# Order and engines of the first image's blocks in a convolution by codebooks: means before shuffles, a patch set before later loads, one pair of numerators on VectorE, one map half through GpSimd's queue

## The chip, the cores and the metric

One core of a Trainium2 chip. The metric is the device time of one execution in microseconds, as the median of several runs. TensorE (PE in the profile), VectorE (DVE), ScalarE (ACT) and GpSimd (POOL) compute; SyncE (SP) only issues transfers. Each engine works through its own instructions in the order in which the program lists them.

## The reference

`x` is 16 images of 256 channels, 28 x 28, in fp32. Cut to what matters:

```python
def amm_conv3x3(x, centroids, w_sub):          # per channel: 16 centroids of 9 values
    p = ...                                    # 3x3 patches: image, position, channel, 9
    d = |p|^2 - 2 p.centroids + |centroids|^2  # distance to 16 centroids of this channel
    attn = softmax(-d)                         # over the 16
    lut = einsum('cks,cso->cko', centroids, w_sub)
    return einsum('bnck,cko->bno', attn, lut)

h = _gn(x)                                     # group norm, 32 groups
out = relu(bn1(amm_conv3x3(h, centroids1, w_sub1)))
out = bn2(amm_conv3x3(out, centroids2, w_sub2))
out = se_layer(out)                            # gate per channel
return x + relu(out + h)
```

## The kernel before, in words

The softmax and the table are taken apart: for each channel the exponentials of the logits are summed against the 9 centroid values (numerators) and against one (denominators), each numerator is multiplied by the reciprocal of its denominator, and the result, 9 values for each channel, goes through an ordinary product with `w_sub`. An image of a layer is four **blocks**: two halves of the channels times two halves of the rows (`BLOCKS`, L46). Two layers of 16 images give 128 blocks, numbered `j` in order; block 0 to 3 are the first image's first layer.

For a block:

- `patches` (L388) loads the shifted rows from a padded map in DRAM, `home1` in the first layer. A block has two patch sets, `p` = 0 and 1, each of six transfers. Sets are counted over all blocks, so the tenth is block 4's second. Two buffers hold them (`pts`; block 1 uses the space of weight slabs, seen as `wall<-home`).
- `logits` (`lg`, L409) and `exps` (`e`, L420): four groups `mm` of a block, TensorE and ScalarE.
- `num_b` (`nb`, L474): the denominators and the ninth numerator. `split_r`, `join_r` (L484, L488), `recip_dve` (L502) make the reciprocal `r`; `split_q`, `join_q` (L494, L499) the ninth numerator.
- `spread` (L513, L517) shuffles `r` to the numerators' rows on VectorE: two shuffles for a group, one for the ninth.
- `num_a` (`na`, L460): the other numerators, one PSUM pair a group. `scale_a` (L536) multiplies them by the spread reciprocals on VectorE, straight from PSUM. Groups in `kept` instead go by `copy_a` (L530, ScalarE) and `scale_q` (L525, GpSimd).
- `product` (L544) multiplies slices `k` of the result by a weight slab, 392 columns at a time. A fp32 matmul is two passes in the profile. The four products of an image's blocks are combined as a seven-multiplication scheme, with `mix` (L551, L553) on GpSimd for its sums and `combine` (L226) for its weights.

Four PSUM pairs of banks are handed on by written rotation (`ROLES`) and, for the first three blocks, by a written table (`EARLY`). A matmul that writes a bank waits for the engine that read it before.

The image's own path: `load_x` reads it into `xt`, one buffer; `gn_stats` (L339, L340) takes the statistics on VectorE; `gn_mean` and `gn_var` each need one small matmul (`gnp`, L345 and L362) and a few VectorE steps (L349 to L353, L364); GpSimd finishes with `rsqrt` (L276, L277) and two steps (L367, L368); `gn_apply` (L374) normalises on ScalarE into `xpads[k]`, where `k` is the half of the channels; `to_home1` (L386) writes it to `home1`, two copies shifted by one. Half 1 of a map is first read by the third block of that image.

The order is written out by hand. `at(cl, sub, f, ...)` files a step under a key, and all steps are issued in the order of the keys; every engine takes its own instructions from that one list. Steps with negative keys are the start. A block's work takes two numbers of `cl`; block 4 begins at 8. Keys that the change touches, before:

- image 1: `load_x` (0, 1.65), `gn_stats` (3, 1.3), block 1's shuffles for groups 1, 2, 3 (3, 1.40 to 1.43), block 0's product in three pieces of 4, 2 and 3 slices (4, 0.80), (4, 0.82), (4, 0.84), with `gn_mean` (4, 0.81) and `gn_var` (4, 0.83) between them;
- block 1's scalings (4, 1.04 on), its kept group 0 copied at (4, 1.05) and scaled on GpSimd at (5, 0.08);
- image 1's `to_home1`: half 0 at (4, 1.6), half 1 at (6, 1.6);
- image 2: `load_x` (6, 2.6), `gn_stats` (8, 0.3); block 3's `join_r` stands at (8, 1.2), its scalings at (9, 1.04);
- block 4's patch sets at (6, 1.5) and (7, 1.5).

Of the kernel before, what the change touches and what calls it, by code (L numbers as in the profile page):

```python
# [17 lines left out]
P = 128  # L18
# [21 lines left out]
SLOT_MM = (1, 0, 2, 3)  # L40
# [43 lines left out]
def kernel(  # L84
# [20 lines left out]
    nc = tc.nc  # L105
# [39 lines left out]
    home1 = [dram.tile([C, 2, HROW], F32, name=f"home1_{b}") for b in range(B)]  # L145
# [116 lines left out]
    xpads = [io.tile([P, NPAD], F32, tag="pc", name="xpad", bufs=4) for _ in range(NB)]  # L262
# [116 lines left out]
    def twice(t):  # L379
        return view(t, 0, [t.ap[0], [1, 2], [1, HROW]])  # L380

    def to_home1(b, k, half=None):
        if k == NB - 1:
            xs.pop(b)
        p0, p1 = (0, P) if half is None else (64 * half, 64 * half + 64)
        nc.sync.dma_start(home1[b][k * P + p0 : k * P + p1], twice(xpads[k][p0:p1]))  # L386

    def patches(u, p):  # L388
        hm = (home1 if u["l"] == 0 else home2)[u["b"]]
# [532 lines left out]
    def at(cl, sub, f, *a, **kw):  # L922
        jobs.setdefault((cl, sub), []).append((f, a, kw))

    def wide_next(j):
        return j + 1 < len(blocks) and blocks[j + 1]["l"] == 1 and blocks[j + 1]["hh"] == 0
# [7 lines left out]
    for j, u in enumerate(blocks):  # L934
        gi, g = 8 * (j // 4), 2 * j
# [12 lines left out]
    for j, u in enumerate(blocks):  # L948
        g = 2 * j
        u["w"] = j  # L950
        wide = u["l"] == 1 and u["hh"] == 0
        for p in range(2):
            u["pt", p] = alts[p] if j == 1 else pts[p]
            if j == 1:
                at(-0.4 if p else -0.9, 0.0, patches, u, p)
            else:
                at(g + p - (2 * NPT if j == 2 else NPT), 1.5, patches, u, p)
            for q in range(2):
                mm = 2 * p + q
                cl, sub = TURN.get((j, mm), (g + p, 0.1 + (0.2 * q if j < 3 else q)))  # L960
                at(cl, sub, logits, u, mm)
                if wide and mm == 0:
                    at(g, 0.12, wide_copy, u, mm)
                    at(g, 0.9, wide_turn, u, mm)
                    at(g, 1.38, wide_max, u, mm)
                    at(g, 1.39, wide_sub, u, mm)
                    at(g + 1, 1.22, wide_back, u, mm)
                    at(g + 1, 1.89, wide_exp, u, mm)
                else:
                    at(cl, 1.06 if (cl, sub) == (4, 1.035) else sub + 0.01, exps, u, mm)  # L970
        kept = SLOT_MM[1 : 4 if wide_next(j) or j == 0 else 2 : 2]
        g = 2 * j + 1 + (j > 2)
        at(g, 1.0, num_b, u)
        at(g, 1.05, split_r, u)
        at(g, 1.2, join_r, u)
        at(g, 1.25, recip_dve, u)
        at(g, 1.3 if j > 1 else 1.06, split_q, u)
        at(g, 1.35 if j > 1 else 1.21, join_q, u)
        g = 2 * j + 2 + (j > 1)
        for i, mm in enumerate(SLOT_MM):  # L980
            at(g, 1.0 + 0.01 * i, num_a, u, mm)
            if mm in kept:
                at(g, 1.05, copy_a, u, mm)
            else:
                at(g - 1, 2.05 if i == 4 - len(kept) and j > 1 else 1.4 + 0.01 * i, spread, u, mm)
                at(g, 1.04 + 0.001 * i, scale_a, u, mm)
        for mm in (4, *kept):
            at(g, 1.2, spread, u, mm)
            at(*((g, 1.3) if j != 1 else (5, 0.06 if mm == 4 else 0.08)), scale_q, u, mm)

    for l in range(2):
        for b in range(B):
            n = l * B + b
            g = 8 * n
            us = blocks[4 * n : 4 * n + 4]
            for c, w, r, ks in PRODUCTS:
                if g + c == 5:
                    for sub, k0, k1 in ((0.8, 0, 4), (0.82, 4, 6), (0.84, 6, 9)):
                        at(4, sub, product, (n, c), us[r], w, ks[k0:k1], k0 == 0, k1 == 9, step=4)
                else:  # L1000
                    at(g + c, 2.0, product, (n, c), us[r], w, ks, step=g + c)
            for mm in (1, 2, 3, 4, 0):
                at(g + 5, 2.5 if n else {4: 0.07, 0: 0.09}.get(mm, 0.05), mix, us[0], mm, us[1], us[0])
                at(g + 7, 1.35 if mm in (4, 0) else 1.25, mix, us[1], mm, us[2], us[1])
                at(g + 8, 1.37 if mm == 1 else 1.4, mix, us[0], mm, us[2], us[0])
                at(g + 10, 1.4, mix, us[0], mm, us[0], us[3])
            c11, c12, c21, c22 = (0, 0), (0, 1), (1, 0), (1, 1)
            at(*((g + 6, 0.0) if n else (4, 0.85)), acc_copy, l, b, c11, (n, 5))
            at(g + 6, 2.02, acc_copy, l, b, None, (n, 6))
            at(g + 8, 0.0, acc_add, l, b, None, (n, 7))  # L1010
            at(g + 8, 2.02, acc_add, l, b, c21, (n, 8), c11)
            at(g + 10, 0.0, acc_add, l, b, c22, (n, 9), c11, pop=False)
            at(g + 10, 0.01, acc_add, l, b, c21, (n, 9))
            at(g + 10, 0.05, reg_add, l, b, c12, c22, None)
            at(g + 10, 0.06, reg_add, l, b, c22, c21, None)
            at(g + 10, 2.02, acc_add, l, b, c12, (n, 10))
            at(g + 12, 0.0, acc_add, l, b, c11, (n, 11))
            at(g + 12, 2.02, acc_add, l, b, c21, (n, 12), op=ALU.subtract)
            if l == 0 or b == B - 1:
                at(g + 11, 1.9, norm_out, l, b, *c12)  # L1020
                at(g + 11, 1.91, norm_out, l, b, *c22)
                at(g + 12, 1.9 if l else 0.05, norm_out, l, b, *c11)
                at(g + 13, 1.06, norm_out, l, b, *c21)
            else:
                for o in range(NB):
                    at(g + 12 + o, 1.9, norm_both, b, o)
            if l == 0:
                for o in range(2):
                    if b == 0:
                        at(g + 13, 1.9, rank_score, o)  # L1030
                        at(g + 13, 1.91, rank_keep, o)
                        at(g + 12 + 2 * o, 0.65 if o else 1.93, h0_keep, o)
                    else:
                        for r in range(2):
                            at(g + 12 + o + (o and r), (0.06, 1.97)[r] if o == 0 else (1.805, 2.9)[r], to_home2, b, o, r)
                if b + 1 < B:
                    at(*((g - 2, 2.6) if b else (0, 1.65)), load_x, b + 1)
                    for q in range(NB):
                        at(*((g, 0.3) if b else (3, 1.3)), gn_stats, b + 1, q)
                    at(*((g + 1, 2.1) if b else (4, 0.81)), gn_mean, b + 1, step=g + 1 if b else 4)  # L1040
                    at(*((g + 3, 2.1) if b else (4, 0.83)), gn_var, b + 1, step=g + 3 if b else 4)
                    for q in range(NB):
                        at(*((g + 4, 1.9) if b else (4, (0.95, 1.055)[q])), gn_apply, b + 1, q)
                        at(*((g + 4, 1.92) if b else (4 + 2 * q, 1.6)), to_home1, b + 1, q)
            else:
                last = b == B - 1
                at(*((g + 11, 0.6) if last else (g + 13, 2.6)), load_x, b, last)
                at(g + 14 - last, 2.1, se_hidden, b, g + 14 - last)
                at(*((g + 14, 1.05, se_gate, b, g + 14) if last else (g + 17, 2.1, se_gate, b, g + 17)))
                at(*((g + 14, 1.05) if last else (g + 18, 0.3)), se_recip, b)  # L1050
                for q in range(NB):
                    at(*((g + 12, 0.4) if last else (g + 19, 1.9)), finish_norm, b, q)
                    if not last:
                        at(g + 18, 1.9, finish_gate, b, q)
                        at(g + 20, 0.05, finish_sum, b, q)
                        at(g + 20, 1.9, finish_relu, b, q)
                        at(g + 20, 2.2, finish_add, b, q)
                        at(g + 20, 2.25, store, b, q)
                    else:
                        at(g + 14, 1.92, finish_fast, b, q)  # L1060
                        at(g + 14, 1.92, store, b, q)
                if b == B - 1:
                    at(g + 11, 1.9, flags)
                    at(g + 12, 2.9, flag_sum)
# [49 lines left out]
    g = 8 * B  # L1114
# [23 lines left out]
    for i in range(2):  # L1138
        to_home1(0, 0, i)
# [18 lines left out]
    with tc.If(rv > 0):  # L1158
        with tc.For_i(0, B, 1) as it:
# [14 lines left out]
            for l in range(2):  # L1174
# [6 lines left out]
                for t2 in range(2):  # L1181
                    us = []
                    for hh in range(2):
                        u = {"l": l, "b": B, "t": t2, "hh": hh, "w": 0, "step": None}
# [127 lines left out]
```

## Time and profile before

| | |
|---|---|
| median of 3 runs | 2630.71 us (2627.92 to 2631.47) |
| profiled execution | 2632.19 us |
| its span, first to last instruction | 2630.7 us |
| TensorE matmul busy | 2587.2 us, 98% |
| VectorE, ScalarE, GpSimd busy | 67%, 52%, 72% |
| mean granted TensorE clock | 0.997 |

A row of a timeline gives start, duration, engine, source line, operation, output<-inputs, shape, count; the bracket at the end is the idle time of the engine before it and what ended it. `gn_st` are the statistics, `gnp` the group matmuls, `qp` and `qo` the numerators (pairs and the ninth), `rb` the spread reciprocals, `xt` the image, `home<-xpad` the map's write, `pt<-home` and `wall<-home` the patches. SPq is SyncE's queue. Neighbouring instructions of one form are merged, with their count.

### The profile page before, as it was taken

What the parts mean: (1) busy time and instruction counts of PE and PEld (TensorE: products, weight loads), DVE (VectorE), ACT (ScalarE), POOL (GpSimd) and SP (SyncE); (2) the same over time, 40 slices, a digit from 0 to 9 for tenths busy, and PEclk for the clock granted to TensorE, in tenths of its full rate; (3) what the DMA queues carried; (4) which work ended last, traced back from release to release, by engine and by line L of the source; (5) the groups of instructions that cost most, each with busy time, mean ns of one, the idle gap of its engine ahead of it and who ended that gap; (6) DMA issues with size and microseconds to landing.
All of it is one profiled execution on the core that took longest, in us unless ns stands there. A gap on an engine that the chain in (4) does not pass through costs nothing.

```text
span 2630.7 us, 85667 instructions
## 1 busy us (share of the span) xinstructions
PE 2587.2 (98%) x36984; PEld 1267.9 (48%) x36984; DVE 1766.0 (67%) x3759; ACT 1360.6 (52%) x1876; POOL 1902.8 (72%) x1320
## 2 busy tenths in 40 slices
PE   6999999999999999999999999999999999999997
PEld 2444454444544445444444444444444444444444
DVE  5776566666567665666666776767776667767665
ACT  4444444445444444444454555555555655555653
POOL 3876667766667766677667777778878787777786
PEclk9999999999999999999999999999999999999999
DMA  8656655665455566655664444444444444444441
GB/s 209 163 154 180 186 162 162 189 182 165 140 147 146 175 184 173 173 151 154 169 168 107 111 116 117 127 115 117 106 126 128 118 118 110 117 119 125 114 121 47
DMA packets 217831, 374.37 MB, mean 142 GB/s; under 512 B 29752, under 2 KB 188008, under 8 KB 217448
## 3 DMA queue, kind: packets, MB, share of 16 engines
q1 hardware_dynamic: 211272, 336.16, 47.8%
q0 software_dynamic: 6176, 32.66, 3.4%
q8 instruction: 295, 4.83, 0.8%
q14 instruction: 88, 0.72, 0.1%
HBM read 288.93 MB, written 79.80 MB: 140 GB/s over the span
## 4 chain that ended last, share of the span: by engine, by line
PE 96%; DMA 2%; DVE 1%; POOL 0%; ACT 0%; SPq 0%; issue 0%; DVEq 0%; POOLq 0%; ACTq 0%
PE acc L544 52%; PE lg L409 17%; PE na L460 14%; PE nb L474 13%; DMA xt<-in_x 1%; DMA wall<-home 1%; DMA pt<-home 0%; PE sep L846 0%; DVE gn_st L339 0%; DVE rb L517 0%; SPq L395 0%; DMA home<-xpad 0%; POOL qp L553 0%; PE sep L835 0%; PE gnp L362 0%
## 5 line engine op out<-in xcount | busy, mean ns | idle before, releaser
L544 PE MATMUL acc<-qp,wall 128*128 128x392 f32 x3072 | 1096.8, 500 | 1.7 <-POOL qp L553 0.9
L420 ACT ACTIVATE e<-lg 128x784 f32<-128x784 f32 x960 | 738.0, 821 | 638.2 <-PE lg L409 635.1
L553 POOL TENSOR_TENSOR qp<-qp,qp 128x784 f32<-128x784 f32 x512 | 944.9, 1869 | 158.6 <-DVE qp L536 158.1
L544 PEld LDWEIGHTS acc<-qp,wall 128*128 128x128 f32 x3072 | 565.2, 190 | 509.1 <-issue 55.3
L517 DVE STREAM_SHUFFLE rb<-r 128x392 f32<-128x392 f32 x1024 | 551.0, 605 | 0.0
L409 PE MATMUL lg<-pt,wd 32*32 32x392 f32 x16256 | 483.4, 502 | 7.3 <-DMA pt<-home 2.7
L488 DVE SCALAR_TENSOR_TENSOR r<-nb,kst,r 128x392 f32<-128x392 f32 x128 | 80.0, 625 | 452.6 <-ACT r L484 438.8
L536 DVE TENSOR_TENSOR qp<-na,rb 128x784 f32<-128x784 f32 x351 | 333.0, 972 | 64.7 <-PE na L460 53.7
L460 PE MATMUL na<-e,cwa 64*32 64x392 f32 x8192 | 374.8, 492 | 0.7 <-DVE hpad L581 0.7
L474 PE MATMUL nb<-e,cwb 64*32 64x392 f32 x8192 | 374.8, 493 | 0.1
L525 POOL TENSOR_TENSOR qo<-qo,rb 128x392 f32<-128x392 f32 x128 | 131.3, 1026 | 314.1 <-DVE rb L513 313.6
L502 DVE RECIPROCAL r<-r 128x392 f32<-128x392 f32 x128 | 333.2, 2603 | 4.4
L525 POOL TENSOR_TENSOR qp<-qp,rb 128x784 f32<-128x784 f32 x161 | 297.9, 1860 | 2.9
L474 PEld LDWEIGHTS nb<-e,cwb 64*32 64x32 f32 x8192 | 192.4, 107 | 174.3 <-issue 19.5
L460 PEld LDWEIGHTS na<-e,cwa 64*32 64x32 f32 x8192 | 182.9, 106 | 183.5 <-issue 76.2
L409 PEld LDWEIGHTS lg<-pt,wd 32*32 32x32 f32 x16256 | 121.2, 103 | 283.1 <-issue 252.1
L544 PE MATMUL acc<-qp,w_A 128*128 128x392 f32 x512 | 183.9, 502 | 0.0
L484 ACT ACTIVATE r<-nb,kst 128x392 f32<-128x392 f32 x128 | 86.7, 677 | 164.0 <-PE nb L474 164.0
L444 POOL TENSOR_TENSOR z<-z,mx 128x1568 f32<-128x1568 f32 x32 | 91.8, 2869 | 94.7 <-DVE mx L438 94.7
L544 PE MATMUL acc<-qo,wall 128*128 128x392 f32 x384 | 157.7, 492 | 0.0
L530 ACT COPY qp<-na 128x784 f32<-128x784 f32 x161 | 130.8, 812 | 27.0 <-PE na L460 25.2
L544 PEld LDWEIGHTS acc<-qp,w_A 128*128 128x128 f32 x512 | 95.0, 191 | 83.0 <-DVE qp L536 19.8
(154 smaller groups left out, 1646.8 us busy)
## 6 DMA issues: line engine op xcount, KB each, us to landing
pt<-home SPq DMA_DIRECT2D x762, 209.0 KB
pt<-home SPq DMA_DIRECT2D x762, 104.5 KB
home<-xpad SPq DMA_DIRECT2D x31, 899.0 KB
xt<-in_x SPq DMA_DIRECT2D x30, 784.0 KB
out_dram<-y SPq DMA_DIRECT2D x32, 392.0 KB
d_wS<-st SPq DMA_DIRECT2D x12, 192.0 KB
wall<-d_wS SPq DMA_DIRECT2D x4, 576.0 KB
wall<-in_ws SPq DMA_DIRECT2D x3, 576.0 KB
```

The costliest lines, as they stand in the source:

```text
L409: nc.tensor.matmul(bk[32 * c : 32 * c + 32, :N].rearrange("p (r w) -> p r w", w=W), lhsT=wts["wd", u["hh"]][32 * i : 32 * i + 32, mm, c, : ...
L420: nc.scalar.activation(eg[:, 2 * i : 2 * i + 2, :], bk[:, :, :N], AF.Exp, scale=2.0)
L444: nc.gpsimd.tensor_tensor(zk, zk, mx.unsqueeze(2).to_broadcast([P, N // 4, K]), ALU.subtract)
L460: nc.tensor.matmul(bs[32 * i : 32 * i + 32, r, :N], lhsT=wts["cwa", u["hh"]][64 * r : 64 * r + 64, mm, i, :], rhs=es[64 * r : 64 * r + 64, ...
L474: nc.tensor.matmul(bs[32 * i : 32 * i + 32, r, :N], lhsT=wts["cwb", u["hh"]][64 * r : 64 * r + 64, mm, i, :], rhs=es[64 * r : 64 * r + 64, ...
L502: nc.vector.reciprocal(u["r"], u["r"])
L517: nc.vector.stream_shuffle(rb[:, r, :], u["r"], mask_of(2 * mm + r))
L525: nc.gpsimd.tensor_tensor(q, q, u.pop(("rb", mm)), ALU.mult)
L530: nc.scalar.copy(pair(u, mm), u.pop(("na", mm))[:, :, :N])
L536: nc.vector.tensor_mul(pair(u, mm), u.pop(("na", mm))[:, :, :N], rb)
L544: nc.tensor.matmul(accs[key][:, :N], lhsT=wl[w][:, k, :], rhs=us["q", k], start=first and n == 0, stop=last and n == len(ks) - 1,)
L553: nc.gpsimd.tensor_tensor(pair(out_u, mm), pair(in0, mm), pair(in1, mm), ALU.subtract)
```

## The change

- `to_home1(0, 1)`, the first image's half 1, is issued by GpSimd instead of SyncE. Its place in the list, before block 1's patches, is unchanged.
- Block 1 keeps no group: group 0 is scaled by VectorE from PSUM like the other three, and its copy on ScalarE and its scaling on GpSimd go. Its two shuffles, which stood after the scalings, join the others.
- Block 1's shuffles move behind the second image's `gn_mean` (group 1's) and behind `gn_var` (the others).
- Block 0's product is cut into 5, 2 and 2 slices.
- The third image's `load_x` moves behind the tenth patch set, and its `gn_stats` from before block 3's `join_r` to just before block 3's scalings.
- Half 1 of the second map is written behind that load.

```diff
@@ to_home1
-        nc.sync.dma_start(home1[b][k * P + p0 : k * P + p1], twice(xpads[k][p0:p1]))
+        eng = nc.gpsimd if (b, k) == (0, 1) else nc.sync
+        eng.dma_start(home1[b][k * P + p0 : k * P + p1], twice(xpads[k][p0:p1]))
@@ blocks
-        kept = SLOT_MM[1 : 4 if wide_next(j) or j == 0 else 2 : 2]
+        kept = () if j == 1 else SLOT_MM[1 : 4 if wide_next(j) or j == 0 else 2 : 2]
...
-                at(g - 1, 2.05 if i == 4 - len(kept) and j > 1 else 1.4 + 0.01 * i, spread, u, mm)
+                if j == 1:
+                    at(4, 0.835 if i else 0.815, spread, u, mm)
+                else:
+                    at(g - 1, 2.05 if i == 4 - len(kept) and j > 1 else 1.4 + 0.01 * i, spread, u, mm)
...
-            at(*((g, 1.3) if j != 1 else (5, 0.06 if mm == 4 else 0.08)), scale_q, u, mm)
+            at(*((g, 1.3) if j != 1 else (5, 0.06)), scale_q, u, mm)
@@ products
-                    for sub, k0, k1 in ((0.8, 0, 4), (0.82, 4, 6), (0.84, 6, 9)):
+                    for sub, k0, k1 in ((0.8, 0, 5), (0.82, 5, 7), (0.84, 7, 9)):
@@ images
-                    at(*((g - 2, 2.6) if b else (0, 1.65)), load_x, b + 1)
+                    at(*((g - 2 + (b == 1), 2.6 - (b == 1)) if b else (0, 1.65)), load_x, b + 1)
                     for q in range(NB):
-                        at(*((g, 0.3) if b else (3, 1.3)), gn_stats, b + 1, q)
+                        at(*((g + (b == 1), 0.3) if b else (3, 1.3)), gn_stats, b + 1, q)
...
-                        at(*((g + 4, 1.92) if b else (4 + 2 * q, 1.6)), to_home1, b + 1, q)
+                        at(*((g + 4, 1.92) if b else (4 + 3 * q, 1.6 + 0.05 * q)), to_home1, b + 1, q)
```

## Prediction

> **What bounds the kernel now.** I read the busy times by stretch first, then the chain that ended last, then each engine's timeline where these two pointed.
>
> ```profile
> 24.00:50.00 26.00, 20.80 (x481) 7.39 (x450) 12.15 (x33) 16.17 (x22) 5.17 (x4) 0.93 0.89 210
> 50.00:80.00 30.00, 26.84 (x369) 11.93 (x347) 21.99 (x53) 13.83 (x20) 14.30 (x12) 0.94 0.79 200
> 80.00:110.00 30.00, 26.64 (x413) 12.21 (x398) 19.79 (x43) 12.10 (x16) 28.95 (x17) 1.00 0.73 198
> 110.00:2580.00 2470.00, 2468.21 (x35528) 1212.40 (x35534) 1675.64 (x3556) 1294.88 (x1787) 1803.28 (x1235) 1.00 0.52 142
> ```
>
> In a row by stretch the second number is TensorE's busy time, the last three are granted clock, DMA share and GB/s. From 110 to 2580 us TensorE stands still for 1.79 us of 2470: nothing can be gained there, and what TensorE gains before 110 us it keeps to the end, since the engines behind it follow it. Before 110 us it stands still for 5.20, 3.16 and 3.36 us, and the diff touches only work between 20 and 110 us. The first two of these rows also show a granted clock below 1.0. So the whole question is which of some 12 us of holes close. The chain names what they hang on.
>
> ```profile
> 10.37 4.15 DMA home<-xpad
> ...
> 42.94 11.03 DMA xt<-in_x
> ...
> 56.36 3.05 DVE rb L517 x6
> ...
> 80.36 12.99 DMA xt<-in_x
> ```
>
> Twice it is an image being loaded, and once six shuffles that stand on VectorE between that image's statistics and its group means.
>
> **Part 1: means ahead of the shuffles, and a longer first piece of the product.** TensorE around 52 to 69 us, in order:
>
> ```profile
> 52.31 2.90 PE L544 MATMUL acc<-qp,w_A 128*128 128x392 f32 x8
> 56.47 0.39 PE L345 MATMUL gnp<-gn_mv,gmat 128*128 128x4 f32 x2 [1.26 <-DVE gn_mv L340]
> 56.72 1.56 PE L544 MATMUL acc<-qp,w_A 128*128 128x392 f32 x4
> 59.95 0.38 PE L362 MATMUL gnp<-gn_dv,gmat 128*128 128x2 f32 x2 [1.67 <-DVE gn_dv L353]
> 61.11 2.82 PE L544 MATMUL acc<-qp,w_A 128*128 128x392 f32 x4
> 63.86 1.02 PE L409 MATMUL lg<-pt,wd 32*32 32x392 f32 x32
> 67.71 1.45 PE L409 MATMUL lg<-pt,wd 32*32 32x392 f32 x32
> 69.10 2.86 PE L474 MATMUL nb<-e,cwb 64*32 64x392 f32 x64
> ...
> 59.30 0.14 DVE L349 COPY gn_gm<-gnp 128x4 f32<-128x4 f32 x1
> 59.55 0.34 DVE L353 SCALAR_TENSOR_TENSOR gn_dv<-gnp,gn_mv,gn_dv 128x1 f32<-128x1 f32 x2
> 60.37 0.16 DVE L364 TENSOR_TENSOR gn_var<-gn_gm,gnp 128x2 f32<-128x2 f32 x1 [0.48 <-PE gnp L362]
> 67.16 1.86 DVE L536 TENSOR_TENSOR qp<-na,rb 128x784 f32<-128x784 f32 x2 [0.34 <-PE na L460]
> 67.41 0.81 ACT L530 COPY qp<-na 128x784 f32<-128x784 f32 x1
> ```
>
> Block 0's product is 18 matmuls (9 slices, two passes each), cut into 8, 4 and 6 with the two group-mean matmuls between. It becomes 10, 4 and 4. One pass takes 2.90 / 8 = 0.36 us. The first piece then ends at 52.31 + 10 x 0.36 = 55.94, where TensorE still waits for the statistics until 56.47: the 1.26 us hole shrinks to 0.5, and two passes move into it. The mean matmuls run to 56.72, the next four passes to 58.17. Meanwhile VectorE, with no shuffles ahead, starts the mean's copy 0.42 us after the matmul (as 59.95 to 60.37), at 56.89, and needs 59.30 to 59.89 = 0.59 us: done at 57.48, before TensorE asks at 58.17. The 1.67 us hole is gone. The second group matmul ends at 58.41, the last four passes at 59.86.
>
> These passes ran slowly before: four took 2.82 us against 1.56. The clock says why.
>
> ```profile
> 57.33:60.75 3.42, 1.75 (x7) 0.85 (x6) 2.69 (x14) 0.00 (x0) 0.14 (x1) 1.00 0.99 201
> 60.75:64.16 3.41, 3.41 (x22) 1.34 (x36) 0.00 (x0) 0.14 (x1) 1.23 (x4) 0.50 0.56 185
> 98.29:101.70 3.41, 1.81 (x48) 0.49 (x48) 3.41 (x11) 1.18 (x2) 3.41 (x3) 1.00 0.62 147
> ```
>
> The stretch with TensorE busy 1.75 of 3.42 us is followed by 3.41 us at half clock, which costs about 1.7 us; a stretch with 1.81 us busy (last row) leaves the full clock. With the hole filled the first stretch is nearly full, so I take the half clock as gone. [...]
>
> The next logits start when the product ends, or when their patches are there. Those are issued behind the image:
>
> ```profile
> 22.55 0.58 SPq L386 DMA_DIRECT2D home<-xpad  x1
> ...
> 36.32 5.83 SPq L395 DMA_DIRECT2D pt<-home  x6
> ...
> 43.88 5.67 SPq L395 DMA_DIRECT2D pt<-home  x6
> ...
> 29.07 2.63 PE L409 MATMUL lg<-pt,wd 32*32 32x392 f32 x64 [2.23 <-DMA pt<-home]
> 37.65 2.75 PE L409 MATMUL lg<-wall,wd 32*32 32x392 f32 x64 [2.30 <-DMA wall<-home]
> ...
> q0 software_dynamic: 160, 0.52, 15.9%
> ```
>
> The last of the six issued from 43.88 on starts about 48.96; with the image's 11.03 us it lands about 59.99, an estimate. So the logits start at 60.1 instead of 63.86: 3.76 us.
>
> **Part 2: block 1's fourth numerator pair on VectorE.** It takes a copy from ScalarE (0.81), a multiplication from GpSimd, and puts one of 1.86 / 2 = 0.93 us and two earlier shuffles on VectorE. VectorE is then: mean done 57.48, two shuffles (3.05 / 6 = 0.51 each) to 58.5, variance at 58.99, six shuffles to 62.04. The first scaling was due 1.03 us after the numerators began; now 60.1 + 0.95 + 1.03 = 62.08, so the shuffles just hide. Four scalings end at 63.0, 63.95, 64.9 and 65.8. The next logits want the second bank at 60.1 + 3.8 + 0.44 = 64.34: in time, where before they waited for ScalarE's copy (the x32 group took 1.45, elsewhere about 0.9). The denominators (69.10) start about 65.0. Parts 1 and 2 together give 4.1 us. If the shuffles run late by 0.3, as much is lost; the GpSimd time freed lies beside TensorE and is worth nothing by itself.
>
> **Part 3: third image's load and statistics later.** The rows around 90 to 104 us:
>
> ```profile
> 90.43 0.94 PE L409 MATMUL lg<-pt,wd 32*32 32x392 f32 x32
> 96.02 1.48 PE L544 MATMUL acc<-qp,wall 128*128 128x392 f32 x4
> 99.48 0.95 PE L409 MATMUL lg<-pt,wd 32*32 32x392 f32 x32 [1.99 <-DVE qo L499]
> 104.08 0.99 PE L409 MATMUL lg<-pt,wd 32*32 32x392 f32 x32
> ...
> 84.60 3.70 SPq L395 DMA_DIRECT2D pt<-home  x6
> ...
> 90.55 0.68 ACT L484 ACTIVATE r<-nb,kst 128x392 f32<-128x392 f32 x1 [1.31 <-PE nb L474]
> 93.37 1.04 DVE L339 BATCH_NORM_STATS2 gn_st<-xt 128x6 f32<-128x392 f32 x2 [5.92 <-DMA xt<-in_x]
> 95.71 0.57 DVE L488 SCALAR_TENSOR_TENSOR r<-nb,kst,r 128x392 f32<-128x392 f32 x1
> 101.32 0.57 DVE L581 TENSOR_TENSOR hpad<-acc,hpad 128x392 f32<-128x392 f32 x1
> 102.81 2.72 DVE L536 TENSOR_TENSOR qp<-na,rb 128x784 f32<-128x784 f32 x3
> ```
>
> In times of before: VectorE stood 5.92 us at the statistics, and the denominators' join, ready at 91.23, came at 95.71. With the statistics moved behind, it starts at 91.25 and the hole of 1.99 us is gone. The chain that took 95.71 to 101.32 ends at 96.86; the accumulator's add must wait for the product's end (97.50), is done about 98.1, and two shuffles bring 99.1. Now come the moved statistics, 93.37 to 95.71 = 2.34 us, ahead of the three scalings: this is a new cost. The first scaling ends at 101.45 + 0.95 = 102.4, and the logits of 104.08, which need its bank, start about 102.6. TensorE alone could have had them at 97.50 + 0.88 + 2.86 = 101.24, so about 1.4 us of the old hole stays as a new one. Gain 1.5 us. It needs the third image landed by 99.1 - 4.1 = 95.0. SyncE's order becomes tenth set, third image, second half of the second map, code table (`c<-in_sk`). The tenth set waits for block 3's logits, so its six issues, 84.60 to 88.30, come at 80.5 to 84.2, and the image's issue at 84.2. At 12.99 us it would land at 97.2, too late by 2.2; but those 12.99 had half a map ahead of them, which now goes behind. I take 9 us, between them and the 4.15 us that a half-size write took in an emptier stage: 93.2, a slack of 1.8. The tenth set lands no later than before, since the image and the map no longer go ahead of it. The map's half is wanted first by block 6's patches, the code table after the first map's last block: neither is on the path.
>
> **Part 4: the first map's other half by GpSimd's queue.** SyncE's twelve issues for block 1 move up by the 0.85 us between 22.55 and 23.40; the transfer itself stays on the same 16 engines, which were busy for 0.89 of 24 to 50 us. The write now shares with block 0's last patches instead of following them: the hole of 2.23 us may grow by the same 2.3 us that the hole of 2.30 us, which waits for all of it, then loses. GpSimd's write waits for ScalarE's normalised map; queued behind it are only the normalisation constants and the clearing of the output maps, which nobody reads before block 0's product ends near 60 us. Sum 0. [...] The bound above is 2.30 us, the hole before block 1's logits. The bound below: GpSimd's queue moved 0.52 MB in the ten microseconds from 79 on (the q0 row); at this rate 0.92 MB take 17.7 us, 22.55 + 17.7 = 40.2, and block 2's patches, which read it and were issued from 36.32, would be 3.9 us late. The half-size write of 4.15 us, twice, gives 30.9: nearer, since that is the same data form and stage.
>
> **Sum.** 4.1 + 1.5 + 0 = 5.6 us. The profiled execution took 2632.19 us (span 2630.7), 1.48 above the median: 2626.6 there, 2625.1 as a median.
>
> **Rivals.**
> - Earlier data: if the lone SyncE queue gains as GpSimd takes its load, all up to the second image comes up to 2.30 us sooner: 2622.8. For it: three holes name DMA. Against: DMA share 0.89 to 0.99.
> - The half clock is not saved, because it does not hang on that hole or because the new hole of 1.4 us brings one: 1.7 less, 2626.8. Against: it follows the emptiest stretch at once, and 3.41 - 1.4 = 2.0 busy is above the 1.81 that kept the clock. [...]
> - The write lands late, at 40.2: 2629.0. The same mechanism gives the slower end: block 2's patches wait for it, one for one, from 36.32 on. Slower than before from a landing at 41.9. At half the q0 rate it lands at 57.9, 21.6 late: 2646.7. Against it: the q0 row comes from a stretch crowded by other transfers.
> - The change does not do what it says: the third image or the shuffles are late again and about 2.2 us is lost: 2627.3.
>
> **How the numbers follow.** Measurement tells about 0.2%, 5.3 us here, from no change; so faster means under 2625.4. Forecast 0.50, its own range 2623.6 to 2626.6, of it 0.38 faster and 0.12 within; earlier data 0.22, faster; half clock 0.08, the late write 0.06 and the third image late 0.04, all within; the slower end 0.10. Faster 0.60, same 0.30, slower 0.10. The range runs from earlier data with 0.5 for spread, 2622.3, to the late write, 2629.0, and leaves out the slow end and little else.
>
> **What would show it.** Right: no hole at the second group matmul, clock 1.00 throughout 53 to 100 us, no wait for `qo L499` near 95 us, a new wait of 1 to 2 us for `qp L536` about five microseconds later, block 0's second patches later and block 1's not. Wrong: SyncE waiting for home at block 2's patches, or a statistics row that waits for the third image.

## The result, and the profile after

The changed kernel took 2625.78 us (median of 14 executions, 2623.59 to 2631.71), the kernel before in the same session 2631.56 (14 executions, 2627.92 to 2637.28). The ratio is 0.9978, 95% interval 0.9970 to 0.9986: 5.8 us less. Forecast were 2625.1 us and a gain of 5.6. That is just beyond the 0.2% that a measurement tells from no change, and the interval reaches to both sides of it.

The profiled execution took 2625.80 us (span 2624.3), 6.39 less than the one of before. Its busy times by stretch, with the columns as before:

```profile
24.00:50.00 26.00, 22.66 (x489) 7.69 (x464) 11.79 (x33) 16.04 (x22) 6.95 (x7) 1.00 0.92 228
50.00:80.00 30.00, 28.42 (x452) 12.45 (x440) 27.30 (x63) 15.80 (x23) 16.93 (x15) 1.00 0.84 226
80.00:110.00 30.00, 28.68 (x429) 14.19 (x430) 18.30 (x44) 12.63 (x19) 29.32 (x19) 1.00 0.61 163
110.00:2580.00 2470.00, 2466.95 (x35453) 1208.53 (x35453) 1676.11 (x3552) 1293.57 (x1786) 1806.26 (x1236) 1.00 0.52 142
```

TensorE's idle time falls from 5.20, 3.16 and 3.36 us to 3.34, 1.58 and 1.32. The granted clock of the second stretch is 1.00 instead of 0.94, and behind 110 us nothing has changed. The 1.00 of the first stretch says little: this profile's clock records begin only at 34.68 us, and the denominators that began at 32.27 took 4.03 us where later ones take 2.86. The lines of code behind `L386` have moved down by one. TensorE's timeline of the changed kernel through parts 1 and 2:

```profile
52.54 3.56 PE L545 MATMUL acc<-qp,w_A 128*128 128x392 f32 x10
56.41 0.38 PE L345 MATMUL gnp<-gn_mv,gmat 128*128 128x4 f32 x2 [0.31 <-DVE gn_mv L340]
56.65 0.91 PE L545 MATMUL acc<-qp,w_A 128*128 128x392 f32 x2
57.39 0.82 PE L545 MATMUL acc<-qo,w_A 128*128 128x392 f32 x2
58.05 0.28 PE L362 MATMUL gnp<-gn_dv,gmat 128*128 128x2 f32 x2
58.19 1.56 PE L545 MATMUL acc<-qp,w_A 128*128 128x392 f32 x4
59.69 0.94 PE L410 MATMUL lg<-pt,wd 32*32 32x392 f32 x32
...
63.41 0.95 PE L410 MATMUL lg<-pt,wd 32*32 32x392 f32 x32
64.34 2.87 PE L475 MATMUL nb<-e,cwb 64*32 64x392 f32 x64
```

The second group matmul (`L362`) has no bracket, so there is no hole ahead of it. The last four passes take 1.56 us where they took 2.82, the second logits 0.95 where they took 1.45. VectorE beside it:

```profile
51.49 2.59 DVE L503 RECIPROCAL r<-r 128x392 f32<-128x392 f32 x1
54.00 0.97 DVE L339 BATCH_NORM_STATS2 gn_st<-xt 128x6 f32<-128x392 f32 x2
...
58.37 0.16 DVE L364 TENSOR_TENSOR gn_var<-gn_gm,gnp 128x2 f32<-128x2 f32 x1
...
61.55 3.62 DVE L537 TENSOR_TENSOR qp<-na,rb 128x784 f32<-128x784 f32 x4
```

The chain that ended last now names VectorE's reciprocal ahead of the statistics, where that of before named the image (42.94 and 11.03 us, so 53.97):

```profile
51.57 2.51 DVE r L503
54.08 0.90 DVE gn_st L339 x2
```

Before, too, the image was late by little. The statistics began 2.74 us behind the reciprocal's start, where they now begin 2.51 behind it, so the image cost 0.23 us:

```profile
51.26 2.59 DVE L502 RECIPROCAL r<-r 128x392 f32<-128x392 f32 x1
```

Around the third image, TensorE's timeline:

```profile
92.37 0.94 PE L410 MATMUL lg<-pt,wd 32*32 32x392 f32 x32
...
97.29 0.95 PE L410 MATMUL lg<-pt,wd 32*32 32x392 f32 x32 [1.13 <-DVE qp L537]
```

and there those of VectorE and of SyncE's queue:

```profile
86.21 0.63 DVE L489 SCALAR_TENSOR_TENSOR r<-nb,kst,r 128x392 f32<-128x392 f32 x1 [3.81 <-ACT r L485]
93.98 1.02 DVE L339 BATCH_NORM_STATS2 gn_st<-xt 128x6 f32<-128x392 f32 x2
96.31 2.69 DVE L537 TENSOR_TENSOR qp<-na,rb 128x784 f32<-128x784 f32 x3
...
83.79 0.38 SPq L175 DMA_DIRECT2D xt<-in_x  x1
```

The logits at 92.37 no longer wait for `qo`, the statistics at 93.98 no longer wait for `xt`, and one new hole of 1.13 us stands before the logits at 97.29.

**Where the 6.4 us are.** TensorE's first 110 us are cut at four of its instructions: the start of block 0's product, block 2's denominators (`nb`, 69.10 before, 64.34 after), the next product's start (`acc`, 91.30 and 86.25), and the one behind it (105.01 and 98.26).

| us | before | after | gain |
|---|---|---|---|
| start of span to block 0's product | 52.31 | 52.54 | -0.23 |
| to block 2's denominators (parts 1 and 2) | 16.79 | 11.80 | 4.99 |
| to the next product | 22.20 | 21.91 | 0.29 |
| to the one behind it (part 3) | 13.71 | 12.01 | 1.70 |
| to the end | 2525.7 | 2526.0 | -0.35 |

The 0.29 and the -0.35 us are not assigned to a part. Within the second cut, the first group matmul (`L345`) is a firmer mark than the product's start. It waits for the statistics, so a product that begins later waits less ahead of it: 4.16 us after the product's start before, 3.87 after. From this matmul to block 2's denominators are 12.63 us before (56.47 to 69.10) and 7.93 after (56.41 to 64.34), a gain of 4.70. The other 0.29 of the 4.99 us mostly give back the 0.23 by which the product began later.

The experiments below are read with the same four cuts, since each part of the change lies within one of them. Executions of one kernel differ by several microseconds (the changed one's lie between 2623.59 and 2631.71), so a whole time tells less than such a cut. Unless said otherwise, a time is the median of 11 executions, with its ratio to the kernel before on the same chip.

### The profile page after: what moved, and what is told of

Read it like the earlier page. It is cut to its first block, busy times and chain, and to the rows that moved or that the text cites. A ratio compares the mean times of both kernels' runs of the same rounds, so it can differ in the third digit from the quotient of the medians.

```text
span 2624.3 us, 85667 instructions
## 1 busy us (share of the span) xinstructions
PE 2585.2 (99%) x36984; PEld 1263.6 (48%) x36984; DVE 1766.3 (67%) x3760; ACT 1360.3 (52%) x1875; POOL 1902.6 (72%) x1320
## 4 chain that ended last, share of the span: by engine, by line
PE 97%; DVE 1%; DMA 1%; SPq 0%; ACT 0%; POOL 0%; issue 0%; DVEq 0%; ACTq 0%; POOLq 0%
PE acc L545 52%; PE lg L410 17%; PE nb L475 14%; PE na L461 14%; DMA pt<-home 0%; SPq L396 0%; DVE rb L518 0%; DVE r L503 0%; PE sep L847 0%; DMA cwa<-in_cwa 0%; DMA home<-xpad 0%; DVE qp L537 0%; ACT e L421 0%; POOL qp L554 0%; DVE gn_st L339 0%
```

## Experiments

### Each part alone

On the kernel before. Parts 1 and 2 alone (`kept`, the shuffles' keys, the pieces):

```diff
+        kept = () if j == 1 else ...            # block 1 keeps no group
+                if j == 1:
+                    at(4, 0.835 if i else 0.815, spread, u, mm)
+                    for sub, k0, k1 in ((0.8, 0, 5), (0.82, 5, 7), (0.84, 7, 9)):
```

> Parts 1 and 2 alone on the kernel before (means ahead of the shuffles, pieces of 5, 2 and 2 slices, block 1's fourth pair on VectorE). By my sum: no hole at the second group matmul, no half clock between 55 and 70 us, third block's denominators start about 65.0 instead of 69.10, 4.1 us less (ratio 0.9984); the hole before qo L499 near 95 us stays at about 2 us. The rival, that the half clock does not hang on that hole: 2.4 us less. The rival that the gain needs the map's write on GpSimd's queue: the second image's statistics no earlier and the patches late, 3 us or less.

2631.55 us, ratio 0.9993 (0.9984 to 1.0002). The second cut takes 11.23 us instead of 16.79, a gain of 5.56 us where the whole change has 4.99, and the old holes at the third image stay. From the first group matmul on it takes 7.84 us, against 7.93 with the whole change: the extra 0.57 us lie ahead of that matmul, which had no wait here because the product began so late. From TensorE's timeline of this run:

```profile
52.62 1.93 PE L409 MATMUL lg<-pt,wd 32*32 32x392 f32 x59 [1.33 <-issue]
55.17 3.56 PE L544 MATMUL acc<-qp,w_A 128*128 128x392 f32 x10 [0.61 <-ACT e L420]
...
96.81 1.20 PE L409 MATMUL lg<-pt,wd 32*32 32x392 f32 x32 [2.31 <-DVE qo L499]
```

The stage gained 5.6 us, but its product began 2.9 us later than in the profile of before, so little of the gain is in the time. The waits shown lie in block 2's first logits and in the product's start, ahead of what the edit reorders; one of them, 1.33 us, has no releaser in the profile.

Part 3 alone (the keys of `load_x`, `gn_stats`, `to_home1` of half 1):

```diff
+                    at(*((g - 2 + (b == 1), 2.6 - (b == 1)) if b else (0, 1.65)), load_x, b + 1)
+                        at(*((g + (b == 1), 0.3) if b else (3, 1.3)), gn_stats, b + 1, q)
+                        at(*((g + 4, 1.92) if b else (4 + 3 * q, 1.6 + 0.05 * q)), to_home1, b + 1, q)
```

> Part 3 alone on the kernel before (third image's load behind the tenth patch set, its statistics before block 3's scalings, second half of the second map behind that load). By my sum: the holes of 1.99 and 0.66 us near 100 us go, a new one of 1.1 to 1.4 us for qp comes about five us later; 1.5 us less (ratio 0.9994), and everything before 85 us as before. The rival, that the third image is late again: the statistics row shows a wait for xt and the gain is 0 or a loss of 1 to 2 us.

2630.81 us, ratio 0.9991 (0.9982 to 1.0000). The second cut stays at 16.80 us, the last takes 12.01 instead of 13.71: the same 1.70 us as in the whole change, with the same new hole:

```profile
102.09 0.95 PE L409 MATMUL lg<-pt,wd 32*32 32x392 f32 x32 [1.13 <-DVE qp L536]
```

Part 4 alone:

```diff
+        eng = nc.gpsimd if (b, k) == (0, 1) else nc.sync
+        eng.dma_start(...)
```

> Part 4 alone on the kernel before (first map's other half on GpSimd's queue). By my sum 0 (ratio 1.0000 within 0.0005): block 1's first logits up to 1.4 us earlier, but block 0's product at the same time, since by the trace of the changed kernel VectorE's reciprocal takes over from the second image as what the statistics wait for. The rival of earlier data: second image's statistics at 52 to 53 instead of 54.0, 1 to 2.3 us less at the end.

2634.00 us, ratio 1.0000 (0.9991 to 1.0009): nothing. Its profile (span 2633.7) tells more about the clock than about the queue. Its TensorE at the two group matmuls:

```profile
59.41 0.39 PE L345 MATMUL gnp<-gn_mv,gmat 128*128 128x4 f32 x2 [0.97 <-DVE gn_mv L340]
62.89 0.38 PE L362 MATMUL gnp<-gn_dv,gmat 128*128 128x2 f32 x2 [1.67 <-DVE gn_dv L353]
63.88 1.48 PE L545 MATMUL acc<-qp,w_A 128*128 128x392 f32 x4
```

and the stretch with that hole and the next one:

```profile
59.65:63.07 3.42, 1.75 (x8) 0.85 (x7) 3.15 (x15) 0.00 (x0) 0.00 (x0) 1.00 0.76 210
63.07:66.48 3.41, 3.41 (x48) 1.57 (x56) 0.16 (x1) 0.63 (x2) 1.37 (x4) 1.00 0.53 163
```

The hole is the one of before, 1.67 us, and its stretch is as empty, 1.75 of 3.42 us; but the next stretch keeps the full clock. With the same hole and no half clock the second cut takes 14.84 us instead of 16.79. Of these 1.95 us, 0.29 lie ahead of the first group matmul, which waited 0.97 us here and 1.26 before. Behind it are 10.97 us (59.41 to 70.38) instead of 12.63, so the half clock costs 1.66 us, and the emptiness of the stretch alone does not bring it. Of the three profiles with this hole, two have the half clock (before, and part 3 alone with 12.61 us behind that matmul) and this one has not.

### Undoing one thing in the changed kernel

The pieces back to 4, 2 and 3 slices, one execution:

```diff
-                    for sub, k0, k1 in ((0.8, 0, 5), (0.82, 5, 7), (0.84, 7, 9)):
+                    for sub, k0, k1 in ((0.8, 0, 4), (0.82, 4, 6), (0.84, 6, 9)):
```

> The changed kernel with block 0's product cut as before, 4, 2 and 3 slices instead of 5, 2 and 2. Theory: the hole before the first group matmul grows by two passes, 0.7 us, to 1.0 if the product starts at 52.5 (and is near 0 if statistics come first); still no hole at the second group matmul, no half clock; product start to third block's denominators 11.8 us plus up to 0.7, against 16.8 before.

2626.95 us. The second cut takes 12.50 us, 0.70 more. The two passes that now stand behind the first group matmul are missing ahead of it, and the timeline shows them as a longer first hole, 0.99 us instead of 0.31:

```profile
56.48 0.39 PE L345 MATMUL gnp<-gn_mv,gmat 128*128 128x4 f32 x2 [0.99 <-DVE gn_mv L340]
```

The longer piece is thus worth 0.7 us where the product waits for the statistics. With parts 1 and 2 alone that matmul had no wait, and there was nothing for it to fill.

Block 1's kept pair back on ScalarE and GpSimd, one execution:

```diff
-        kept = () if j == 1 else SLOT_MM[...]
+        kept = SLOT_MM[...]
-            at(*((g, 1.3) if j != 1 else (5, 0.06)), scale_q, u, mm)
+            at(*((g, 1.3) if j != 1 else (5, 0.06 if mm == 4 else 0.08)), scale_q, u, mm)
```

> The changed kernel with block 1's group 0 kept on ScalarE and GpSimd as before, its two shuffles behind the scalings. Theory: the other three scalings are due when their numerators come, the x32 logits after block 1's numerators take 1.3 to 1.5 us again instead of 0.95 as they wait for the copy, so 0.3 to 0.5 us more from the product's start to the third block's denominators. Rival: GpSimd's extra 1.9 us delays block 0's mix and a hole for qp or qo comes in the accumulation near 70 us.

2629.49 us. The second cut takes 12.25 us. From its first logits to the denominators are 5.08 us instead of 4.65, because the second logits wait for the copy's bank again:

```profile
61.02 0.95 PE L410 MATMUL lg<-pt,wd 32*32 32x392 f32 x32 [0.48 <-DMA pt<-home]
64.73 1.44 PE L410 MATMUL lg<-pt,wd 32*32 32x392 f32 x32
66.10 2.86 PE L475 MATMUL nb<-e,cwb 64*32 64x392 f32 x64
```

So the fourth pair on VectorE is worth 0.43 us, by this one execution. The other losses of this execution are waits for patches (0.48 us here, 1.32 in the third cut) and a later first product (53.85); whether they come from the edit, one execution can't tell.

### The clock

In the kernel before, only the order of block 1's shuffles is changed: four stay ahead of the means, two go behind the second group matmul. One execution.

```diff
+                if j == 1:
+                    at(*((4, 0.835) if i == 3 else (3, 1.4 + 0.01 * i)), spread, u, mm)
```

> The kernel before with only the last two of block 1's six shuffles moved behind the second image's means: the hole at the second group matmul shrinks from 1.67 to about 0.65 us. Theory, the half clock hangs on a window that is less than about half busy: no half clock near 60 to 64 us, so product start to third block's denominators falls from 16.8 by 1.0 + 1.9 to about 13.9. Rival, the half clock comes from something else: 15.8.

2631.91 us. The hole at the second group matmul is 0.69 us and no half clock follows; the second cut takes 13.86 us:

```profile
59.78 0.38 PE L362 MATMUL gnp<-gn_dv,gmat 128*128 128x2 f32 x2 [0.69 <-DVE gn_dv L353]
```

By itself this agrees with the prediction's reading that the half clock hung on that hole. Beside part 4 alone, where the whole hole brought none, it proves little. In the same execution the third image's hole of 2.49 us left a stretch with 0.92 us busy, and the next one ran at 0.50, where the profile of before had kept the full clock:

```profile
95.20:98.61 3.41, 0.92 (x19) 0.34 (x32) 3.41 (x6) 0.48 (x1) 3.41 (x3) 1.00 0.77 195
98.61:102.03 3.42, 3.42 (x64) 0.84 (x40) 3.42 (x11) 1.54 (x2) 3.42 (x3) 0.50 0.09 28
```

The second try went at the half clock near 40 us, which some executions show. Four useless matmuls were put into the two holes ahead of it, on a kernel that also has the next section's edit:

```diff
+    def keep_warm(tag, n):      # n matmuls of wd into a bank that is free there
+    at(1, 0.09, keep_warm, 0, 2)
+    at(2, 0.09, keep_warm, 1, 2)
```

> The version before this one (changed kernel, third image's statistics behind the scalings) with four matmuls of no use, two ahead of block 0's second logits and two ahead of block 1's first, where TensorE otherwise waits for patches. Theory: the time to block 0's product, 52.0 to 55.5 us over the profiles so far in both kernels, hangs on whether one of those holes falls into a window that halves the clock. Then no half clock shows after 34 us, the product starts by 52.5, and the median falls by 1 to 2 us against the same kernel without them. Rival: patches and VectorE's chain set the product's start; then nothing is gained and up to 1 us lost.

2630.36 us, ratio 0.9989 (0.9980 to 0.9998). This failed: the half clock near 40 us was there all the same (39.39 to 46.21; the numerators took 5.15 us instead of 2.86), block 0's product began at 56.14, later than in any other profile, and there was another half clock behind a stretch that was busy for 2.52 us:

```profile
53.04:56.45 3.41, 2.52 (x65) 0.88 (x34) 2.45 (x4) 3.21 (x6) 0.00 (x0) 1.00 0.92 223
56.45:59.87 3.42, 3.42 (x6) 1.66 (x5) 3.35 (x7) 0.68 (x1) 0.00 (x0) 0.50 1.01 238
```

### The remaining hole, and the queue once more

The new hole of 1.13 us was forecast as the price of the statistics ahead of the scalings. In the changed kernel they are put behind them:

```diff
-                        at(*((g + (b == 1), 0.3) if b else (3, 1.3)), gn_stats, b + 1, q)
+                        at(*((g + (b == 1), 1.1 if b == 1 else 0.3) if b else (3, 1.3)), gn_stats, b + 1, q)
```

> The changed kernel with the third image's statistics moved on, from before block 3's scalings to behind them (key 1.1 instead of 0.3). If the new hole of 1.13 us at the logits near 97 us is those 2.34 us of statistics standing ahead of the scalings, it goes, and the kernel takes 1.1 us less than the changed one (ratio to before about 0.9974). The rival, that the statistics then delay the next shuffles and GpSimd's scalings, brings the hole back one step later, at the accumulation near 98 to 105 us: no gain.

2626.80 us, ratio 0.9979 (0.9970 to 0.9988). The hole is gone, and the last cut takes 10.71 us instead of 12.01:

```profile
98.81 0.94 PE L410 MATMUL lg<-pt,wd 32*32 32x392 f32 x32
99.68 4.22 PE L545 MATMUL acc<-qp,wall 128*128 128x392 f32 x12
```

It was then measured again on one chip with the changed kernel and with both of them writing the first map's half from SyncE:

```diff
-        eng = nc.gpsimd if (b, k) == (0, 1) else nc.sync
-        eng.dma_start(...)
+        nc.sync.dma_start(...)
```

> The changed kernel once more, so that the next three can be compared with it on one chip. By the sum 5.6 us under the one before (ratio 0.9979).

> The changed kernel with the third image's statistics behind block 3's scalings, once more beside the changed one. By its first trace the stretch from block 4's S3 product to its S2 product takes 10.71 us instead of 12.01, so 1.2 us under the changed kernel. Rival: the gain is lost again later: same as the changed kernel.

> The changed kernel with the first map's other half written by SyncE again (part 4 undone). My theory, part 4 is worth 0: the median of the changed kernel within 1 us; block 1's patches issued 0.6 to 0.9 us later. Rival of earlier data: 1 to 2.3 us slower than the changed kernel, as the second image lands that much later and is then what the statistics wait for.

> The same with the first map's other half written by SyncE. Theory, the two are independent and part 4 is worth nothing: same as n1_again, 1.2 us under the changed kernel. Rival: 1 to 2.3 us above n1_again.

| us (ratio to before, 2633.57) | GpSimd's queue | SyncE's queue |
|---|---|---|
| statistics before the scalings | 2628.82, 0.9983 (0.9974 to 0.9992) | 2629.54, 0.9986 (0.9977 to 0.9995) |
| statistics behind the scalings | 2628.55, 0.9980 (0.9971 to 0.9989) | 2627.22, 0.9979 (0.9970 to 0.9988) |

By queue the means are 2628.7 and 2628.4: part 4 is worth nothing here that these runs resolve. By place of the statistics they are 2629.2 and 2627.9, 1.3 us less. That these means agree with the last cut is partly luck. The medians differ by 0.27 us with GpSimd's queue and by 2.32 with SyncE's, while the cut goes from 12.01 to 10.72 us and from 12.00 to 11.31; the forecast 1.2 us is in the cut of the first pair, but not in its median. The intervals do not settle it. No time here shows the version with the statistics behind the scalings as worse than the changed kernel, with either queue. In the profile with SyncE's queue a new wait takes part of the cut's gain, by its bracket for GpSimd's sums for the product:

```profile
97.42 4.11 PE L544 MATMUL acc<-qp,wall 128*128 128x392 f32 x12 [0.52 <-POOL qp L553]
```

## Why the prediction was right

**Parts 1 and 2: forecast 4.1 us, measured 4.99 from product start to denominators, 4.70 of it behind the first group matmul.** The mechanism is shown: both holes behaved as written (1.26 to 0.31 against a forecast 0.5; 1.67 to none), and parts 1 and 2 alone gave the same stage. By the experiments the 4.70 us are 1.66 of half clock (forecast 1.7), 1.67 of hole, 0.68 of longer pieces and 0.43 of the fourth pair, 4.44 in all; 0.26 are not assigned. The last two rest on one execution each.

The denominators came at 64.34, 0.66 us sooner than the forecast 65.0. Three steps make this up:
- The statistics ended 0.06 us sooner.
- From the first group matmul to the next logits the sum had 3.63 us, up to patches that land at 59.99. The logits came after 3.28 us, at 59.69, without a bracket: the patches were no bound here. (With block 1's pair kept they were, by 0.48 us.)
- From these logits to the denominators the sum had 4.9 us, and 4.65 were measured. Its own terms, 3.8 + 0.95, end at 64.85; "about 65.0" rounds up.

VectorE also ran ahead of the sum, at no gain. The sum has the variance wait 0.48 us for the second group matmul. The variance at 58.37 follows the shuffles without a bracket, since that matmul was done at 58.05 + 0.28 = 58.33, while they ran. So the scalings started at 61.55 instead of 62.08, but already in the sum they were ready in time for TensorE.

**Part 3: forecast 1.5 us, measured 1.70.** The chain was right at each link. The join started at 86.21 without the statistics ahead of it, the image was there when they came at 93.98, issued at 83.79 (forecast 84.2), and the hole for `qp` was 1.13 us (forecast 1.4). That it is the statistics' place that makes this hole is shown by moving them. The load's new place was not tried apart from theirs.

**Part 4: forecast 0, and no gain or loss measured, but by another way than written.** The sum let the hole of 2.23 us grow by what the hole of 2.30 us loses. No run shows this: the two holes are 2.39 us and none in the profile after, 2.47 and 2.54 with part 4 alone. The write on GpSimd, in the profile after:

```profile
22.06 0.80 POOL L387 DMA_DIRECT2D home<-xpad  x1 [1.39 <-ACT xpad L374]
```

and TensorE's timeline behind it:

```profile
29.03 3.30 PE L410 MATMUL lg<-pt,wd 32*32 32x392 f32 x64 [2.39 <-DMA pt<-home]
32.27 4.03 PE L475 MATMUL nb<-e,cwb 64*32 64x392 f32 x64
36.30 1.80 PE L410 MATMUL lg<-wall,wd 32*32 32x392 f32 x48
38.44 0.89 PE L410 MATMUL lg<-wall,wd 32*32 32x392 f32 x16 [0.34 <-ACT e L421]
44.44 1.77 PE L410 MATMUL lg<-wall,wd 32*32 32x392 f32 x32 [0.45 <-DVE qp L537]
51.72 0.89 PE L410 MATMUL lg<-pt,wd 32*32 32x392 f32 x16 [0.97 <-DVE qo L500]
```

Block 0's second patches were not late (29.03 against 29.07 before), though the prediction names their being late as a sign that it is right, and block 1's logits started at 36.30 without a wait instead of 37.65. So data did come earlier, as the rival of earlier data had it. But the 1.35 us went again before the product: waits of 0.34, 0.45 and 0.97 us for ScalarE and VectorE, which had become the late ones.

The chain says how much there was to gain. From the end of block 0's denominators it runs through ScalarE's split and VectorE's join, reciprocal, shuffles and first scaling to block 1's last logits and denominators, and through the next split and joins to the product. It takes 16.24 us here (36.30 to 52.54). It takes 16.25 or 16.26 in four more profiles, one of them with SyncE's queue, although block 1's logits start up to 1.35 us behind those denominators there. In the profile of before they start 2.30 us behind, and it takes 16.96 (35.35 to 52.31); with part 3 alone 2.11 us behind, and it takes 16.76. In before:

```profile
31.63 3.72 PE L474 MATMUL nb<-e,cwb 64*32 64x392 f32 x64
```

So about 0.7 of the wait of 2.30 us lay on the path, and not the 2.30 that the rival counts. The changed kernel's profile has this 0.7, but its denominators of block 0 begin 0.64 us later and take 4.03 us instead of 3.72, and the product begins 0.23 later. An earlier image alone could not have helped by more than the 0.23 us that it had cost. In the other profiles with this edit the wait before block 1's logits is anything from none to 2.60 us, and with SyncE's queue from 0.68 to 2.42, so even the earlier start is not a steady effect.

**The clock.** The conclusion was right (no half clock between 53 and 100 us), the reading behind it was not. The prediction took 1.75 us of 3.42 as too empty and 1.81 as enough; part 4 alone had 1.75 and kept the clock, and the run with the useless matmuls lost it behind 2.52. Up to 110 us the recorded stretches at half clock are 3.41 or 6.83 us long, and they do not begin at a fixed place in the kernel: at 30.03 and 60.75 us in the profile of before, at 37.17 and 98.61 with four shuffles ahead, at 39.39 and 56.45 with the useless matmuls. In the 3.41 us just ahead of these six TensorE was busy for 0.92 to 2.52 us. What decides is open. One thing stands out if the stretches at full clock are taken as 3.41 us long too, which the 27.31 us between the two half clocks of before (33.44 to 60.75, 8 x 3.41) allow: the two profiles that have the half clock behind the hole of 1.67 us have their stretches at the same place, with an edge at 60.75 us, and the hole begins 0.95 and 0.69 us into its stretch; with part 4 alone it begins 1.57 us into it. That would fit a dependence on where the hole lies in its stretch, but three profiles don't show one, and it was not tried apart. Filling this hole went with the full clock behind it in every profile that had it filled.

**Rivals.** A late write and a late third image did not occur in the changed kernel. That the half clock would not be saved did not occur either, but the price of 1.66 us is that of an execution in which it strikes; the old hole brought it in two of three profiles. With part 4 alone, where the patches still stand behind the other loads, one profile has a wait for patches of 3.24 us at the third image. Part 3's order may take such waits away; no run shows that it does:

```profile
101.97 1.24 PE L410 MATMUL lg<-pt,wd 32*32 32x392 f32 x32 [3.24 <-DMA pt<-home]
```

**The whole time.** That it came within 0.2 us of the forecast gain is partly luck. In the profiles the gain is 6.4 us, 0.8 more than the sum; the medians differ by less because the profiled execution of before was 0.6 us slower than the median of its session. Single executions of the changed kernel lie between 2623.59 and 2631.71 us. Measured again on another chip the change is worth 4.75 us (0.9983), and the three parts alone, each to within some 2.4 us, add up to 3.5.

## What to carry to other kernels

Where whole times scatter by several microseconds, compare the stage between two fixed instructions of the bounding engine, and begin it at one that waits for the chain in question. From the product's start, the stage of parts 1 and 2 took 11.2 to 12.9 us in the eight profiles that had them whole; from the first group matmul, which ends the wait for the statistics, 7.83 to 7.94. When a step is moved out of one chain, price it in the chain where it comes to stand: the third image's statistics left the join and stood before the scalings, and only behind those did TensorE no longer wait for what they delayed. A transfer that lands sooner is worth something only while it is the last to arrive; here VectorE and ScalarE stood right behind it, and of a wait of 2.30 us only 0.7 was to be had.

## What the runs showed that was not expected

Block 0's product began anywhere from 52.04 to 56.14 us in fourteen profiles, and two profiles of one kernel (statistics behind the scalings) differ by 2.6 us there. The fourteen fall into three groups. In seven, the profiles of before and after among them, it began between 52.04 and 53.03. In four, TensorE ran at half clock for 6.83 us, beginning between 37.2 and 39.4 us, and it began between 53.41 and 56.14. The two profiles of one kernel are one of these four and one of the seven; the numerators at half clock and at full clock:

```profile
40.88 5.23 PE L461 MATMUL na<-e,cwa 64*32 64x392 f32 x64
```

```profile
39.93 2.86 PE L461 MATMUL na<-e,cwa 64*32 64x392 f32 x64
```

In the last three, TensorE stops for 0.74 to 1.93 us behind five of block 2's first logits, released by nothing that the profile shows, and the product began between 53.85 and 55.17. Both lie ahead of block 0's product, and what is lost there is not made up later. What brings them on was not settled. Only one execution of each run was profiled, so how often the others fall into each group can't be read, nor how much of a median's difference comes from that.
